# Reordering the opening of a two-block transformer kernel: modulation in column parts, four heads first, setup spread over the first batch

## The chip, the core and the metric

The kernel runs on one core of a Trainium2 chip. A core has five engines with a queue each: TensorE (PE, matrix products; PEld is its weight load), VectorE (DVE), ScalarE (ACT), GpSimd (POOL) and SyncE (SP), which here only issues DMA transfers. Each engine takes its instructions strictly in order; engines wait for one another by semaphores. The metric is the device time of one execution in microseconds (us), lower is better; the time of the kernel before is the median of three runs.

## The reference

Two transformer blocks run one after the other on x of shape 8 x 512 x 256 (8 batches, 512 tokens, 256 features, 16 heads), all in fp32. The opening, which the change touches, computes this of block 0:

```python
mod = jax.nn.silu(c) @ adaln_w.T + adaln_b            # 8 x 2304
shift_sa, scale_sa, gate_sa, shift_ca, scale_ca, gate_ca, shift_ff, scale_ff, gate_ff = jnp.split(mod, 9, axis=-1)
h = modulate(ln(x), shift_sa, scale_sa)               # x * (1 + scale) + shift
q = ln(_heads(h, H)) * qn_w + qn_b                    # head size 16, no projection
k = ln(_heads(h, H)) * kn_w + kn_b
v = _heads(h, H)
attn = jax.nn.softmax(jnp.einsum('bhqd,bhkd->bhqk', q, k) * scale, axis=-1)
x = x + gate_sa[:, None, :] * _unheads(jnp.einsum('bhqk,bhkd->bhqd', attn, v))
h = modulate(ln(x), shift_ca, scale_ca)
kv = brain_tokens @ cond_w.T + cond_b                 # 8 x 64 tokens of context
# cross attention of h with keys and values of kv, gated by gate_ca; then a gated feed-forward
```

Block 1 has self-attention with rotary positions and head size 64, cross attention with a layer-normed context (its keys and values, too, are made early, during block 0), and a feed-forward. Its two modulations are linear in the same condition vector: `g = c @ gw + gb`, four of them side by side (8 x 1024).

## The kernel before

x of all batches stays in SBUF, in 4 tiles of 128 tokens per batch. Block 0 is one software pipeline over **slots**: `run_blocks` (line 52) walks a list of `blocks`, and in each slot i emits first the scores of block i (`score`, 4 heads of one key tile: PE products into two pairs of PSUM banks, then two exponentials on ACT), then the values of block i - 1 (PE, into `ps_O`), then everything that `at(i, fn)` has registered for slot i, in the order of registration. A batch has 16 such self-attention blocks in a cycle of 18 slots (`CYCLE`); slots 9 and 13 of each cycle are left for the two blocks of cross attention of the batch before (`batch2`), and two cycles behind runs the feed-forward (`batch3`). So cycle 0 holds the self-attention of batch 0 and, in its gaps, the setup; cycle 1 holds batch 1, the cross attention of batch 0 and the keys of block 1 (`keys1`).

Heads go in groups of four: group g covers every second head of half c = g // 2 of the features (`c, par = divmod(g, 2)`). `queries_keys(g)` (line 472) transposes the normalized rows `z` on PE; ACT makes q, DVE makes k of it. It stands two slots before its group's first block. Its rows come from a chain of steps: `norm` (layer norm and modulation), `head_centre` (head mean subtracted, DVE), `head_var` (square on ACT, sum on DVE), `head_scale` (power -0.5 and product, POOL). For batch 0 these are registered in slots -1 to 1, for a later batch ten to four slots ahead of its first block, always ahead of the setup steps of the same slot, because the batches are registered first (line 690) and the setup after them.

PSUM: `bank_s` gives two buffers for scores; `bank_o` one for values; `bank_x` (line 99) hands out three banks in turn (two named ps_X, one ps_D) for everything else. Who asks for a bank waits until its last reader is done.

The setup: `linear_rows` (line 253) multiplies an 8-column stationary by 512 columns of weights, `to_columns` (260) transposes such rows in pieces of 128. `modulation` (slot 1), `context0` (3), `keys0` (5), `values0` (7 to 10), the layer norm of the context (5), `modulation1` (12) and `context1` (14) make the tables that cycle 1 needs. `awake(n)` (266) is n products of no use that keep PE busy while it waits for data. `rstd_of` (171) computes powers on POOL. The DRAM row `modd` holds the modulation, and `spread` (352) reads rows of it back, broadcast over the 128 partitions.

The order of PE, DVE, ACT and POOL inside `run_blocks` is the order of emission (`manual_schedule`, line 789); what stands ahead of it, and SP's queue everywhere, is ordered by the framework's planner. `keys1(p)` (730) stands in slots 20, 22, ... 34, and stores its result to DRAM at once (737); the cross attention's denominators take a way over DRAM on the same SP queue: `rec<-den` (616), `rec<-rec` (625), `rb<-rec` (627), after which DVE scales (630) what the output projection `w_o` reads on PE.

## Time and profile before

| what | value |
|---|---|
| median of 3 runs | 2475.15 us (2473.76 to 2475.49) |
| the profiled execution: its time, its span | 2477.8 us, 2476.0 us |
| granted TensorE clock, mean | 0.991 |
| PE, DVE, ACT, POOL busy, share of the span | 98%, 43%, 35%, 35% |
| first scores (slot 0) start | 25.07 us |
| slot 18 (first of cycle 1) starts | 100.40 us |
| clock at half in the first 200 us | 23.7 to 34.0, 85.2 to 92.0, 180.7 to 187.6 us |

How to read it: all times are from the span's start. In the timeline a row is start, duration, engine, line, operation, out<-in, shapes, count, and in brackets how long the engine had stood idle and what ended that. A row can merge several instructions of one kind. Line 109 is the helper `mm`, so matmuls are told apart by their tiles: `ps_S<-q,k` are scores, `ps_O<-p,h` values, `ps_X<-adaw,scT` the modulation. One fp32 product counts as two instructions. SPq rows are DMA issues. The clock is the share of the full TensorE clock that was granted.

### The profile page before, as it was taken

How to read it: one execution, taken by the hardware profiler on the slowest of the kernel's cores; microseconds unless marked ns; L12 is line 12 of the kernel's file. 1: busy time of each engine (PE TensorE's matmuls, PEld its weight loads, DVE VectorE, ACT ScalarE, POOL GpSimd, SP SyncE). 2: the span in 40 equal slices, each digit the busy share in tenths (PEclk: the TensorE clock that was granted, in tenths of full speed). 3: DMA queues.
4: the chain of work that ended last, by engine and by line, in shares of the span. 5: the costliest groups of instructions: out<-in, count | busy, mean ns of one | idle time of the engine just before them, and what ended most of it. 6: DMA issues, size and time to landing. Idle time of an engine off the chain costs nothing.

```text
span 2476.0 us, 28331 instructions
## 1 busy us (share of the span) xinstructions
PE 2414.9 (98%) x10938; PEld 1154.0 (47%) x10938; DVE 1070.0 (43%) x2073; ACT 876.7 (35%) x1115; POOL 857.8 (35%) x537
## 2 busy tenths in 40 slices
PE   8999999999999899999999999999999999999999
PEld 3323444434435543444444444444445555566666
DVE  4555435444434434343434343435343666651120
ACT  3555545555452124333333333333332121212221
POOL 3452322332301025343434343434343454441110
PEclk9999999999999999999999999999999999999999
DMA  5120000000002000000000000000113221211000
GB/s 183 36 82 24 17 11 12 21 11 12 13 11 79 10 1 23 19 18 19 18 18 19 18 19 18 19 18 18 36 61 95 66 67 51 76 42 41 18 21 23
DMA packets 84432, 84.33 MB, mean 34 GB/s; under 512 B 42400, under 2 KB 58720, under 8 KB 84280
## 3 DMA queue, kind: packets, MB, share of 16 engines
q1 hardware_dynamic: 83672, 81.88, 10.5%
q8 instruction: 88, 1.44, 0.2%
q10 hardware_dynamic: 616, 0.55, 0.1%
q14 instruction: 56, 0.46, 0.1%
HBM read 72.36 MB, written 10.04 MB: 33 GB/s over the span
## 4 chain that ended last, share of the span: by engine, by line
PE 93%; DVE 2%; ACT 2%; POOL 1%; issue 1%; DMA 0%; SPq 0%; POOLq 0%; DVEq 0%; ACTq 0%
PE ps_X L109 37%; PE ps_S L109 24%; PE ps_D L109 16%; PE ps_O L109 13%; PE ps_X L362 1%; ACT p L498 1%; DVE t L716 1%; POOL q L717 1%; PE ps_X L478 0%; PE ps_X L520 0%; ACT hT L363 0%; POOL rstd L469 0%; DVE t L713 0%; DVE st L183 0%; PE ps_D L478 0%
## 5 line engine op out<-in xcount | busy, mean ns | idle before, releaser
L109 PE MATMUL ps_S<-q,k 32*128 32x512 f32 (+1 forms) x3072 | 432.2, 627 | 7.0 <-ACT p L498 3.4
L886 ACT ACTIVATE p<-ps_S 128x1024 f32<-128x1024 f32 x256 | 248.2, 1022 | 522.2 <-PE ps_S L109 522.2
L498 ACT ACTIVATE p<-ps_S 128x1024 f32<-128x1024 f32 x256 | 248.2, 1021 | 259.6 <-PE ps_S L109 258.7
L109 PEld LDWEIGHTS ps_S<-q,k 32*128 32x128 f32 (+1 forms) x3072 | 160.2, 185 | 244.5 <-issue 134.3
L865 DVE TENSOR_TENSOR t<-ps_X,rope_c 128x512 f32<-128x512 f32 x126 | 87.1, 692 | 349.9 <-PE ps_X L109 349.9
L905 DVE TENSOR_TENSOR sm<-sm,p 128x1024 f32<-128x1024 f32 x128 | 191.4, 1539 | 59.0 <-ACT p L886 59.0
L175 POOL TENSOR_TENSOR rstd<-rstd,mhalf 128x4 f32<-128x4 f32 x49 | 49.8, 1016 | 392.4 <-DVE rstd L174 391.6
L868 POOL TENSOR_TENSOR q<-t 128x512 f32<-128x512 f32 x32 | 40.7, 1272 | 388.7 <-DVE t L866 388.7
L901 POOL TENSOR_TENSOR sm<-p 128x1024 f32<-128x1024 f32 x64 | 149.4, 2359 | 38.4 <-ACT p L886 38.4
L109 PE MATMUL ps_X<-hT,w 128*128 128x512 f32 x344 | 160.4, 601 | 1.6 <-DVE t L671 1.1
L717 POOL TENSOR_TENSOR q<-t,t 128x512 f32<-128x512 f32 x72 | 94.4, 1311 | 185.7 <-DVE t L716 170.9
L109 PE MATMUL ps_O<-p,h 128*32 128x512 f32 x1024 | 139.0, 615 | 0.5 <-ACT oT L511 0.5
L109 PE MATMUL ps_O<-p,v 128*64 128x512 f32 x512 | 138.0, 617 | 0.0
L109 PE MATMUL ps_D<-p,v 128*64 128x512 f32 x512 | 131.6, 592 | 0.0
L109 PE MATMUL ps_X<-hT,w_sa_wq 128*128 128x512 f32 x256 | 115.9, 595 | 3.0 <-ACT hT L363 3.0
L109 PE MATMUL ps_X<-w_sa_wv,hT 128*128 128x512 f32 x256 | 118.0, 604 | 0.0
L389 DVE TENSOR_TENSOR x<-ps_X,x 128x512 f32<-128x512 f32 x27 | 18.7, 691 | 225.0 <-PE ps_X L109 224.9
L109 PE MATMUL ps_X<-w_sa_wo,oT 128*128 128x256 f32 x512 | 114.5, 382 | 0.1
L109 PE MATMUL ps_X<-hT,w_sa_wk 128*128 128x512 f32 x248 | 112.4, 596 | 0.0
L109 PE MATMUL ps_S<-hT,w_ff_w 128*128 128x512 f32 x256 | 111.3, 592 | 0.0
L469 POOL TENSOR_TENSOR rstd<-var,mhalf 128x32 f32<-128x32 f32 (+1 forms) x17 | 87.3, 5134 | 68.3 <-ACT t L670 41.7
L109 PEld LDWEIGHTS ps_X<-w_sa_wo,oT 128*128 128x128 f32 x512 | 96.0, 190 | 24.2 <-issue 11.4
(252 smaller groups left out, 3542.4 us busy)
## 6 DMA issues: line engine op xcount, KB each, us to landing
rb<-rec SPq DMA_DIRECT2D x128, 128.0 KB
rb<-rec_d SPq DMA_DIRECT2D x124, 128.0 KB
x<-in_x_dram SPq DMA_DIRECT2D x8, 512.0 KB
rb<-rec SPq DMA_DIRECT2D x16, 256.0 KB
out_dram<-x SPq DMA_DIRECT2D x16, 256.0 KB
bc<-modd SPq DMA_DIRECT2D x8, 384.0 KB
gate<-modd SPq DMA_DIRECT2D x16, 128.0 KB
k_d<-q SPq DMA_DIRECT2D x8, 256.0 KB
```

The lines of the kernel that those rows point to most:

```text
L109: nc.tensor.matmul(o, lhsT, rhs, start=start, stop=stop)
L175: nc.gpsimd.tensor_tensor(r[:, :n], r[:, :n], mhalf[:, :n], ALU.pow)
L362: nc.tensor.transpose(ps[:, t * P : (t + 1) * P], z[:, t, k * P : (k + 1) * P], ident)
L469: nc.gpsimd.tensor_tensor(r, s["var", c][:, :, hd], half, ALU.pow)
L498: nc.scalar.activation(pr[u], pss[u], AF.Exp, scale=HD0 ** -0.5)
L716: nc.vector.tensor_tensor(t2[d], ps[src], sn[src].to_broadcast([64, *shape[1:]]), ALU.mult)
L717: nc.gpsimd.tensor_tensor(dst, t1, t2, ALU.add)
L865: nc.vector.tensor_tensor(c, ps, rope_c, ALU.mult)
L868: nc.gpsimd.tensor_tensor(r[0], ec, os, ALU.subtract)
L886: nc.scalar.activation(pr, pss[u], AF.Exp, scale=HD1 ** -0.5)
L901: nc.gpsimd.tensor_tensor(sm, s["p", g, 0, u], s["p", g, 1, u], ALU.add)
L905: nc.vector.tensor_tensor(s["sm", g, u], s["sm", g, u], s["p", g, t, u], ALU.add)
```

## The change

The opening is emitted in program order for PE, DVE, ACT and POOL (`ms` is entered ahead of it). x of batch 0 is loaded in four pieces, the first 512 columns of the modulation weights from ACT's queue, the rest and the biases (now in 4 + 1 pieces) from SP's. The first two modulation rows are made on PE for all 128 partitions at once (`sc0` is the condition of batch 0, repeated over 128 columns), bias and the added one included, where before a row was computed, added on DVE and spread by a product with ones. `awake` gets 6 and 16 products instead of 4 and 13.

Batch 0's steps up to the first scores are done for the first group of four heads alone, at half the width of before, with the last scaling on DVE; the other four heads of the half follow in slots 0 and 1, the second half in slots 2 to 4. `first_mod` is read until slot 2. `z` of batch 0 is filled with zeros as a whole.

`modulation` computes its first 2048 columns as four parts of 512 in four 32-column strips of PE (stationary `sc32`, 32 columns of which 8 are used); the last 256 are `modulation_end`; `modulation1` does the same with four parts of 256 and `c32`. Transposes, `context0`, `keys0` and `values0` become single pieces over slots 3 to 15. Fills on POOL move into slots 5 and 6. For batch 0 only the gate is spread, in slot 6; x of batch 1 is loaded earlier. Key stores of block 1 move from `keys1(p)` to three slots later, with three buffers instead of two, and `open_ff` (the feed-forward's weights) to two slots later.

The diff, cut to its core (`context0(m)`, `keys0(m)`, the columns' slices and the `par` argument of `head_centre` and `head_var` are as their names say):

```diff
     def load_rest():
         load_k(ctxT, a["ctxT"], 96)
         load_k(condw, a["cond_wT"], 96)
+        for j in range(4):
+            nc.sync.dma_start(gb[32 * j : 32 * j + B, :], a["gb_b"][:, D * j : D * j + D].to_broadcast([B, D]))
         nc.sync.dma_start(ctx_in, a["ctx"].rearrange("(t p) d -> p t d", p=P))
         load_k(wk0, a["wkT"])
+        load_x(1)
         load_k(wv0, a["wvT"])
         nc.sync.dma_start(rows, a["rows"].to_broadcast([P, 5 * D]))
-        nc.sync.dma_start(gb, a["gb_b"].to_broadcast([B, 4 * D]))
         load_k(gbw, a["gb_w"])
         load_k(w_q0, a["wqT"])
         load_k(w_o0, a["woT"])
-        for b in range(1, B):
+        for b in range(2, B):
             load_x(b)
 
-
-    scT = sp.tile([P, 2, B], F32, name="scT")
...
+    first_mod = bank_x()
+    ms = ExitStack()
+    ms.enter_context(tc.manual_schedule(engines={ENG.PE, ENG.DVE, ENG.Activation, ENG.Pool}))
+    nc.sync.dma_start(cT, a["cT"].rearrange("(k p) b -> p k b", p=P))
+    for k in range(2):
+        nc.scalar.dma_start(adaw[:, k, 0 : 2 * D], a["adaln_wT"][k * P : (k + 1) * P, 0 : 2 * D])
+    for t in range(NT):
+        nc.sync.dma_start(xs[0][:, t, :], a["x"][0][t * P : (t + 1) * P, :])
+    nc.vector.memset(mod, 0.0)
+    nc.vector.memset(gb, 0.0)
+    nc.gpsimd.memset(hs[0][:, :, :, HD0 + 1 : 32], 0.0)
+    nc.gpsimd.memset(hs[0][:, :, :, HD0 : HD0 + 1], 1.0)
+    nc.gpsimd.memset(sc32, 0.0)
+    nc.gpsimd.memset(c32, 0.0)
+    for j in range(4):
+        nc.sync.dma_start(mod[32 * j : 32 * j + B, 0 : 2 * D],
+                          a["adaln_b"][:, 2 * D * j : 2 * D * j + 2 * D].to_broadcast([B, 2 * D]))
+    nc.sync.dma_start(mod[0:B, 2 * D :], a["adaln_b"][:, 8 * D :].to_broadcast([B, D]))
+    nc.sync.dma_start(cols, a["cols"])
+    load_k(adaw[:, :, 2 * D :], a["adaln_wT"][:, 2 * D :])
+
     nc.scalar.activation(scT, cT, AF.Tanh, scale=0.5)
     nc.vector.scalar_tensor_tensor(scT, scT, 1.0, cT, ALU.add, ALU.mult)
     nc.vector.tensor_scalar_mul(scT, scT, 0.5)
-
-    def linear_rows(dst, xT, w, lo, n):
-
+    nc.vector.tensor_copy(sc0, scT[:, :, 0:1].to_broadcast([P, 2, P]))
+    awake(6)
+    for k in range(2):
+        mm(first_mod, sc0[:, k, :], adaw[:, k, 0 : 2 * D], k == 0, False)
+    mm(first_mod, ones, mod[0:1, 0 : 2 * D], False, False)
+    mm(first_mod[:, D : 2 * D], ones, chk[0:1].rearrange("p i c -> p (i c)"), False, True)
+    awake(16)
+
+    def modulation():
+
+        ps = bank_x()
+        for k in range(2):
+            for j in range(4):
+                mm(ps[32 * j : 32 * j + 32, :], sc32[:, k, :], adaw[:, k, 2 * D * j : 2 * D * j + 2 * D], k == 0, k == 1)
+        nc.vector.tensor_tensor(mod[:, 0 : 2 * D], ps, mod[:, 0 : 2 * D], ALU.add)
+        nc.vector.tensor_scalar_add(mod[0:B, D : 2 * D], mod[0:B, D : 2 * D], 1.0)
+        for j in range(4):
+            nc.sync.dma_start(modd[:, 2 * D * j : 2 * D * j + 2 * D], mod[32 * j : 32 * j + B, 0 : 2 * D])
+
+    def modulation_end():
+        ps = bank_x()
+        for k in range(2):
+            mm(ps[:32, :D], sc32[:, k, :], adaw[:, k, 8 * D :], k == 0, k == 1)
+        last = mod[0:32, 2 * D :]
+        nc.vector.tensor_tensor(last, ps[:32, :D], last, ALU.add)
+
+        nc.vector.tensor_scalar_mul(last, last, 0.5)
+        nc.sync.dma_start(modd[:, 8 * D :], mod[0:B, 2 * D :])
+
...
-    awake(4)
-    linear_rows(mod, scT, adaw, 0, 512)
-    nc.vector.tensor_scalar_add(mod[:, SC_SA : SC_SA + D], mod[:, SC_SA : SC_SA + D], 1.0)
-    first_mod = bank_x()
-    mm(first_mod, ones, mod[0:1, 0 : 2 * D])
-    linear_rows(mod, scT, adaw, 512, 256)
-    nc.sync.dma_start(modd[:, 0 : 3 * D], mod[:, 0 : 3 * D])
-    awake(13)
...
-    def modulation():
-        for lo in range(3 * D, 9 * D, 512):
-            linear_rows(mod, scT, adaw, lo, 512)
-
-        nc.vector.tensor_scalar_mul(mod[:, G_FF : G_FF + D], mod[:, G_FF : G_FF + D], 0.5)
-        nc.sync.dma_start(modd[:, 3 * D :], mod[:, 3 * D :])
-        to_columns(modT, mod, [lo + k * P for lo in (SH_CA, SC_CA, SH_FF, SC_FF) for k in range(2)])
-        for lo in (2, 6):
-            nc.vector.tensor_scalar_add(modT[:, lo : lo + 2, :], modT[:, lo : lo + 2, :], 1.0)
...
     def modulation1():
 
-        for lo in range(0, 4 * D, 512):
-            linear_rows(gb, cT, gbw, lo, 512)
-        gbT = sp.tile([P, 8, B], F32, name="gbT")
-        to_columns(gbT, gb, [k * P for k in range(8)])
+        ps = bank_x()
+        for k in range(2):
+            for j in range(4):
+                mm(ps[32 * j : 32 * j + 32, :D], c32[:, k, :], gbw[:, k, D * j : D * j + D], k == 0, k == 1)
+        nc.vector.tensor_tensor(gb, ps[:, :D], gb, ALU.add)
+
+    def modulation1_columns():
+        ps = bank_x()
+        for k in range(2):
+            nc.tensor.transpose(ps[:, k * P : (k + 1) * P], gb[:, k * P : (k + 1) * P], ident)
+        nc.vector.tensor_copy(gbT.rearrange("p (j k) b -> p k j b", j=4),
+                              ps[:, :D].rearrange("p (k j r) -> p k j r", k=2, j=4)[:, :, :, 0:B])
+
...
+        def first_modulated(c, par=None):
+
+            lv = parts(s["ln"], c, par)
+            n = lv.shape[2]
+            hv = s["hv"][:, :, 8 * c : 8 * c + 8] if par is None else s["hv"][:, :, 8 * c + par : 8 * c + 8 : 2]
+            sh, sc = (parts(first_mod[:, None, i * D : (i + 1) * D], c, par).to_broadcast([P, NT, n, HD0])
+                      for i in range(2))
+            nc.vector.tensor_tensor(lv, lv, sc, ALU.mult)
+            nc.vector.tensor_tensor(hv, lv, sh, ALU.add)
+
+        def head_rows():
+            s["z"] = wk.tile([P, NT, DX], F32, tag="zx", name="zx", bufs=1)
+            nc.gpsimd.memset(s["z"][:, :, D if b else 0 : DX], 0.0)
+
...
+        def head_scale(c, par=None, eng=None):
+            var, z = s["var", c, par], parts(s["z"][:, :, 0:D], c, par)
+            n = z.shape[2]
             half = mhalf[:, 0 : NT * n].rearrange("p (t h) -> p t h", t=NT)
-            nc.gpsimd.tensor_tensor(r, s["var", c][:, :, hd], half, ALU.pow)
-            nc.gpsimd.tensor_tensor(zv, zv, r[:, :, :, None].to_broadcast([P, NT, n, HD0]), ALU.mult)
+            nc.gpsimd.tensor_tensor(var, var, half, ALU.pow)
+            (eng or nc.gpsimd).tensor_tensor(z, z, var[:, :, :, None].to_broadcast([P, NT, n, HD0]), ALU.mult)
...
-                        at(-1, lambda: norm(0))
-                        at(-1, lambda: head_centre(0))
-                        at(-1, lambda: head_var(0))
-                        at(-1, lambda: head_scale(0, 0))
-                        at(0, lambda: head_scale(0, 1))
-                        at(0, lambda: norm(1))
-                        at(0, lambda: head_centre(1))
-                        at(1, lambda: head_var(1))
-                        at(1, lambda: head_scale(1))
+                        def before():
+                            head_rows()
+                            norm()
+                            nc.vector.tensor_copy(qk_cols, cols[:, 0:2])
+                            first_modulated(0, 0)
+                            head_centre(0, 0)
+                            head_var(0, 0)
+                            head_scale(0, 0, nc.vector)
+
+                        def gate():
+                            spread(s["bc"][:, 2 * D : 3 * D], b, G_SA, D)
+
+                        at(-1, before)
+                        at(0, lambda: first_modulated(0, 1))
+                        at(0, lambda: head_centre(0, 1))
+                        at(1, lambda: head_var(0, 1))
+                        at(1, lambda: head_scale(0, 1))
+                        at(2, lambda: first_modulated(1))
+                        at(3, lambda: head_centre(1))
+                        at(4, lambda: head_var(1))
+                        at(4, lambda: head_scale(1))
+                        at(6, gate)
...
+    at(0, lambda: nc.vector.tensor_copy(sc32[:, :, 0:B], scT))
     at(1, modulation)
-    at(3, context0)
-    at(5, keys0)
-    for t in range(4):
-        at(7 + t, lambda t=t: values0(t))
-    at(12, modulation1)
-    at(5, lambda: layernorm(ctx_z, ctx_in, EPS1, 4, CD))
-    at(14, context1)
+    at(3, modulation_columns)
+    at(3, modulation_end)
+    at(4, lambda: context0(0))
+    at(5, lambda: context0(1))
+    at(6, lambda: nc.gpsimd.memset(vb0, 0.0))
+    at(7, lambda: keys0(0))
+    at(8, lambda: keys0(1))
+    for h in hs[1:]:
+        at(5, lambda h=h: nc.gpsimd.memset(h[:, :, :, HD0 + 1 : 32], 0.0))
+        at(5, lambda h=h: nc.gpsimd.memset(h[:, :, :, HD0 : HD0 + 1], 1.0))
+    for t, i in enumerate((9, 9, 11, 12)):
+        at(i, lambda t=t: values0(t))
+    at(9, lambda: layernorm(ctx_z, ctx_in, EPS1, 4, CD))
+    at(12, lambda: nc.vector.tensor_copy(c32[:, :, 0:B], cT))
+    at(13, modulation1)
+    at(13, context1)
+    at(14, modulation1_columns)
+    at(15, modulation1_end)
...
-        q = kv1["pool"].tile([P, N], F32, tag="q", name="q")
+        kv1[p] = q = kv1["pool"].tile([P, N], F32, tag="q", name="q", bufs=3)
         rope_pair(kv1["pool"], ps.rearrange("p (j n) -> p j n", j=B), kv1["rope_c"][:, None, :], kv1["rope_s2"][:, None, :],
                   [P, B, T], q.rearrange("p (j n) -> p j n", j=B))
-        nc.sync.dma_start(k_d[:, p], q.rearrange("p (b t) -> p b t", b=B))
+
+    def store_keys1(p):
+        nc.sync.dma_start(k_d[:, p], kv1[p].rearrange("p (b t) -> p b t", b=B))
...
-    at(2 * CYCLE, open_ff)
+        at(CYCLE + 5 + 2 * p, lambda p=p: store_keys1(p))
+    at(2 * CYCLE + 2, open_ff)
```

## The prediction, made before the result was known

> **What bounds the kernel now.** I read the page first (busy shares, chain), then PE's busy time and granted clock in short windows, then the timeline of the first 190 us.

> ```profile
> PE 2414.9 (98%) x10938; PEld 1154.0 (47%) x10938; DVE 1070.0 (43%) x2073; ACT 876.7 (35%) x1115; POOL 857.8 (35%) x537
> ...
> PE 93%; DVE 2%; ACT 2%; POOL 1%; issue 1%; DMA 0%; SPq 0%; POOLq 0%; DVEq 0%; ACTq 0%
> ```

> PE bounds nearly all of it, so an edit of the opening pays only where PE stands still, runs at half clock, or does less. Windows (length; PE, PEld, DVE, ACT, POOL busy; granted clock; DMA):

> ```profile
> 20.31:23.72 3.41, 0.66 (x4) 0.42 (x4) 0.00 (x0) 0.33 (x1) 3.33 (x3) 1.00 0.97 345
> 23.72:27.13 3.41, 2.06 (x8) 0.52 (x8) 2.82 (x5) 0.45 (x1) 2.40 (x2) 0.50 1.04 384
> 27.14:30.55 3.41, 2.30 (x12) 1.00 (x8) 0.82 (x2) 2.10 (x3) 0.00 (x0) 0.50 1.10 351
> 81.75:85.16 3.41, 1.39 (x7) 0.36 (x5) 3.34 (x6) 0.00 (x0) 0.00 (x0) 1.00 0.00 0
> 85.16:88.58 3.42, 3.35 (x16) 1.21 (x20) 2.09 (x14) 0.83 (x2) 0.00 (x0) 0.50 0.00 0
> 180.74:187.56 6.82, 6.82 (x26) 2.76 (x26) 1.86 (x4) 2.65 (x3) 5.04 (x2) 0.50 1.04 366
> 1890.80:1894.21 3.41, 2.24 (x5) 0.93 (x6) 2.95 (x5) 0.00 (x0) 1.91 (x3) 1.00 0.00 0
> 1894.21:1897.62 3.41, 3.41 (x14) 2.25 (x13) 1.55 (x3) 1.61 (x2) 2.73 (x3) 1.00 0.02 4
> ```

> A window in which PE was busy 0.66 or 1.39 of 3.41 us is followed by clock 0.50; one with 2.24 is not. Half clock then lasts 6.8 to 10.2 us (23.72 to 33.96, 85.16 to 91.99, 180.74 to 187.56). The way to the first scores, in the timeline:

> ```profile
> 7.12 0.43 DVE L183 BATCH_NORM_STATS2 st<-x 128x6 f32<-128x256 f32 x1 [1.85 <-DMA x<-in_x_dram]
> ...
> 14.30 0.69 DVE L434 TENSOR_TENSOR ln<-ln,ps_X 128x512 f32<-128x512 f32 x1 [0.98 <-PE ps_X L109]
> ...
> 19.04 2.90 POOL L469 TENSOR_TENSOR rstd<-var,mhalf 128x16 f32<-128x16 f32 x1 [8.27 <-DVE var L460]
> ...
> 22.70 0.66 PE L478 MATMUL ps_X<-ident,zx 128*128 128x128 f32 x4 [3.06 <-POOL zx L470]
> ...
> 25.07 2.09 PE L109 MATMUL ps_S<-q,k 16*128 16x512 f32 x8 [1.72 <-DVE k L482]
> ```

> Call the scores of slot i S(i). S0 starts at 25.07; further down the same timeline S2 at 39.53, S12 at 76.23, S18 (the next batch) at 100.40. The two later stalls:

> ```profile
> 80.83 0.67 DVE L450 TENSOR_REDUCE mean<-h 128x32 f32<-128x512 f32 x1
> ...
> 84.63 0.41 PE L263 MATMUL ps_D<-ident,gb 8*128 8x8 f32 x4 [1.90 <-DVE gb L258]
> ...
> 171.53 2.50 POOL L717 TENSOR_TENSOR q<-t,t 128x512 f32<-128x512 f32 x2
> 172.84 0.33 SPq L737 DMA_DIRECT2D k_d<-q  x1
> 173.25 0.38 SPq L625 DMA_DIRECT2D rec<-rec  x1
> ...
> 179.82 2.06 PE L109 MATMUL ps_D<-w_o,oT 128*128 128x256 f32 x6 [3.23 <-DVE oT L630]
> ```

> At 84.63 PE waits for DVE, which is centring heads of the next batch. At 179.82 it waits for DVE's scaling, that for a DMA, and SP issued its forerunner only after a key store that waited for POOL.

> **The change part by part.** I laid the queues of PE, ACT, DVE and POOL out by hand from S0 to S18 in the listing's order, each instruction starting when its engine is free and its input there, with the durations of this execution: S 1.07 (2.04 where its second bank waits for the exponentials), values 1.0, exponentials 1.94, transposes 0.59, k 0.81, one centring 1.58. The old order, laid out alike, gives S18 at 102.5 against 100.40 in the trace: 2.1 too long over 75 us, so I take 1.0 off the new one.

> *1. To S0.* x arrives in four pieces of its own and behind less: 0.9 earlier by bytes ahead of it at 384 GB/s (estimate; bounds 0 and 1.7), so 6.2. Statistics of the last piece 0.6, then 1.32 over POOL and 1.38 scaling as before, with waits: normalized at 9.7. The modulation rows now come straight from PE: awake(6) is 12 instructions of 0.43 at half clock from 1.45 (the identity is done at 1.40), to 6.6; four of 0.43 to 0.86, two alike, two of 0.22 end at 9.2 to 10.5. So DVE's first product starts at 9.9, not 14.30. From there 10.77 led to S0; five DVE steps of half width cost 0.42, not 0.69 (1.35 less), the square 0.41, not 0.63, the scaling on DVE 0.42, not POOL's 0.62: 9.0. S0 at 18.9; awake(16), 32 x 0.216 = 6.9, ends at 16.1 to 17.4 where the transposes want 16.5. I take 19.0: **-6.1** (-4.5 to -6.6). POOL's fill of z (1088 columns at 1.77 per 2048: 0.95) and the two ACT issues ahead of its table load (0.43 each) lie under awake(6). SP issues 32 transfers to S0 instead of 26, at 0.43 about 14 us in all, under the same 19; none waits there for the modulation any more (8.6 us at line 278).

> *2. S0 to S2.* Modulation was 12 matmuls of 0.43 and transposes on PE; four column parts run together as the values do (8 instructions per 1.0), so 16 cost 2.0. S1 waits 2.2 for the exponentials, then 2.04 + 1.0 + 2.0: 7.2 instead of 14.46, **-7.2** at full clock. But between the first transposes (end 17.4) and S0 PE idles 1.7, then 1.1 before S1: a 3.41 window over this holds 1.1 to 1.8 busy, between the rows 1.39 and 2.24. I expect half clock (65 in 100; where the windows lie is not mine to choose): **+3.1** from the layout; 0 is the other end, 5.1 (10.24 us at half) the far one.
> [...]

> *3. S2 to S12.* Nine scores and nine values (18.6), four transposes (2.4) and setup (context 3.44, keys 3.44, three values0 2.58, columns 0.59, last part 0.86) make 31.9, about what it was. S11 waits for its exponentials as before (1.1 + 1.0). New are the waits: the transposes of slot 2 for POOL's 2.9 power of half block two (0.9), of slot 6 for its 5.44 one (1.1), and the second values0 of slot 9 for a bank that keys0(1) leaves only once DVE, busy with the next batch's layernorm (2.43 + 1.12 + 1.38), has read it (2.0). 31.9 + 6.1 = 38.0 instead of 36.7: **+1.3** (0 to +3).

> *4. S12 to S18.* A wait takes the place of the old one. c32's copy stands last in slot 12 on DVE: behind k (0.81), two centrings (3.16) and values0's four additions (1.2). modulation1, first in slot 13 after the values, needs it; the context transposes and S14 queue behind it. q ends 1.3 after the transposes; DVE's 5.3 then outlast PE's 0.86 + 1.0: PE idles **4.8** (3 to 5). That is over a window, so half clock follows as at 85.16, costing 2.7 (2.0 to 3.4). modulation1 itself falls from 8 x 0.43 to 1.0. Matmuls and usual waits 18.1 + 4.8 + 2.7 = 25.6 instead of 24.1: **+1.5** (-2.5 to +2.5).

> *5. Key stores.* Stored three slots later, they no longer stand before rec: it goes when DVE's reciprocal is done (170.57), not at 173.25. rb then lands about 2.7 earlier; PE waits 0.9 instead of 3.23 (2.3 saved), and no window falls under 1.4, so 6.82 at 0.50, wholly busy, costs 3.4 less: **-5.7** (0 to -6.6). The third buffer of q lets POOL write before the store; open_ff two slots later leaves six slots of over 5 us to up(0), which used hT from 209.20, 33 us after the weights' issue at 176.17. From here to 766 PE has no gap over 0.3, so what is gained stays.

> *At nothing:* the fill of vb0 (1.80) and of the second h on POOL in slots 5 and 6, behind the scaling of slot 4 and before values0 in slot 9; gate's spread in slot 6, used in slot 19; the five stores of modulation, behind the loads on SP, first read in slot 8; w_ck's load, freed by DVE's last setup product in slot 15, some 8 us before S18 as now (92.36). Without that cover they would come onto POOL's and SP's queues, where the power of slot 14 (two of 5.44) is next in line and its transposes have under 1 us to spare.

> *Sum:* -6.1 - 7.2 + 3.1 + 1.3 + 1.5 - 5.7 - 1.0 = -14.1. The profiled execution took 2477.8 (span 2476.0), 2.65 over the median: 2463.7, and on the median's footing **2461.0**.

> **Rivals.** *A: no half clock at the start* (window falls well; 1.7 idle only): 2461.0 - 3.1 = 2457.9. *B: DVE keeps up*: c32 comes early enough that PE stops under 2 us, no half clock at slot 13; against it k alone waits for ACT. 2.8 + 2.7 better: 2455.5, with A 2452.4. *C: the key-store stall stays*, since POOL's power (5.42) is the same and SP may find another wait: +5.7, 2466.7; with the late ends of 1 (+1.6) and 3 (+1.7), 2470.0. *D: within 0.2%*: C so, with the far ends of 2 (+2.0) and 4 (+1.0) as well, 2473. *E, slower:* the clock stays at half. Windows with 2.06 and 2.30 busy did not lift it. If cycle 0's sparse slots (S on 16 rows, waits for ACT) keep it there, each window costs up to 1.7; nine windows, 31 us or S0 to S8, eat the 14.1, and twelve give 2461.0 + 20.4 = 2481. Against it: at half clock the same work fills windows, as 30.55 to 33.96 did.

> **How the numbers follow.** Forecast with half clock at the start and the c32 wait 40, A 22, B 13, C 12, D 8, E 5 in 100. Leaving out E, D's upper half and a little of B's far end: 2450 to 2470. 0.2% (4.95 us) is about what a measurement of this kernel tells from no change: under 2470.2 is faster 0.87, D same 0.08, E slower 0.05.

> **What would show it.** S0 at 18.9 to 19.8; PE idle near 1.7 before it, and whether clock 0.50 follows; modulation's 16 matmuls in about 2.0; PE waiting 3 to 5 us for DVE's c32 before modulation1, with 0.50 after it; S18 near 92; no wait of 3 us before w_o's matmuls, and full clock after them. I am wrong if DVE's order in slot 12 is not the listing's, if ACT's queue brings the weights later than 7 us, or if rec waits for POOL again.

## The result, and the profile after

The changed kernel takes 2471.45 us (median of 20 executions, 2465.9 to 2478.21). The kernel before, executed beside it, takes 2477.91 (20 executions, 2473.76 to 2484.3). The ratio is 0.9972, 95% interval 0.9963 to 0.9980: faster by 0.28%, 6.5 us, where 14.1 were forecast. The median of three from which the forecast was counted, 2475.15, lies 2.8 under that of the twenty, so the forecast is compared as a difference. The executions spread over 12 us.

The profiled execution took 2471.62, span 2469.8, clock 0.990. The page's first and fourth part:

```profile
PE 2410.8 (98%) x10952; PEld 1154.1 (47%) x10952; DVE 1065.5 (43%) x2083; ACT 877.3 (36%) x1116; POOL 856.6 (35%) x538
...
PE 92%; DVE 2%; POOL 2%; issue 2%; ACT 1%; DMA 0%; SPq 0%; POOLq 0%; DVEq 0%; ACTq 0%
```

PE bounds it as before. The way to the first scores, and slots 13 to 15, in the timeline (start, duration, engine, line, operation, count, idle before and what ended it):

```profile
9.98 0.42 DVE L477 TENSOR_TENSOR ln<-ln,ps_X 128x256 f32<-128x256 f32 x1
...
13.23 2.90 POOL L506 TENSOR_TENSOR var<-var,mhalf 128x16 f32<-128x16 f32 x1 [4.77 <-DVE var L500]
...
19.10 1.38 PE L109 MATMUL ps_S<-q,k 16*128 16x512 f32 x8 [1.72 <-DVE k L519]
...
75.78 1.19 DVE L342 TENSOR_TENSOR vb<-ps_D,rows 64x128 f32<-64x128 f32 x4
...
76.98 0.18 DVE L759 COPY c<-cT 128x16 f32<-128x16 f32 x1
...
77.25 1.35 PE L109 MATMUL ps_X<-gbw,c 128*32 128x256 f32 x16 [4.57 <-issue]
...
83.16 2.38 PE L109 MATMUL ps_S<-q,k 16*128 16x512 f32 x8 [0.37 <-ACT p L535]
```

S0 starts at 19.10 instead of 25.07, and PE waits 4.57 us for c32's copy, which DVE reaches at 76.98. PE's windows (length; PE, PEld, DVE, ACT, POOL busy; granted clock; DMA) show what follows:

```profile
16.46:19.88 3.42, 1.71 (x15) 0.90 (x13) 1.70 (x5) 0.78 (x1) 0.00 (x0) 1.00 1.08 374
19.88:23.29 3.41, 2.32 (x10) 1.00 (x8) 1.09 (x4) 1.94 (x2) 0.00 (x0) 0.50 1.00 377
...
74.49:77.90 3.41, 0.65 (x12) 0.50 (x16) 3.25 (x11) 1.18 (x2) 0.00 (x0) 1.00 0.01 2
77.90:81.32 3.42, 3.42 (x20) 1.97 (x16) 2.85 (x6) 0.00 (x0) 3.28 (x1) 0.50 0.02 5
81.32:84.73 3.41, 3.04 (x22) 1.24 (x14) 2.03 (x9) 2.28 (x3) 3.33 (x3) 1.00 0.00 0
84.73:88.14 3.41, 3.41 (x16) 0.72 (x16) 1.60 (x11) 1.71 (x2) 3.41 (x1) 0.50 0.10 26
...
98.38:101.80 3.42, 3.42 (x18) 0.72 (x16) 0.00 (x0) 2.48 (x3) 0.00 (x0) 0.50 0.00 0
101.80:105.21 3.41, 3.41 (x16) 0.92 (x12) 0.00 (x0) 1.94 (x2) 0.00 (x0) 0.50 0.00 0
105.21:108.62 3.41, 3.41 (x23) 1.35 (x23) 1.00 (x5) 2.14 (x3) 2.27 (x1) 1.00 0.02 5
```

The clock is half from 19.88 to 30.12, from 77.90 to 81.32, and then from 84.73 to 105.21, six windows in which PE was occupied throughout. The window ahead of these six had PE occupied for 3.04 of 3.41 us and no gap above 0.37. Where the gain stands, by the starts of slots:

| slot | before | after | gain |
|---|---|---|---|
| S0 | 25.07 | 19.10 | 6.0 |
| S2 | 39.53 | 29.77 | 9.8 |
| S12 | 76.23 | 68.10 | 8.1 |
| S18 | 100.40 | 96.15 | 4.3 |
| S20 | 106.27 | 105.25 | 1.0 |
| S37 | 173.19 | 171.86 | 1.3 |
| S39 | 188.91 | 184.72 | 4.2 |

Nearly all is lost between S12 and S20. From S37 to S39 it grows by 2.9, because the clock was not halved near 180 this time. The stall there is still in place:

```profile
170.21 2.50 POOL L780 TENSOR_TENSOR q<-t,t 128x512 f32<-128x512 f32 x2
...
171.52 0.32 SPq L802 DMA_DIRECT2D k_d<-q  x1
...
171.93 0.38 SPq L676 DMA_DIRECT2D rec<-rec  x1
...
172.74 0.32 SPq L802 DMA_DIRECT2D k_d<-q  x1
...
178.85 1.56 PE L109 MATMUL ps_X<-w_o,oT 128*128 128x256 f32 x6 [3.58 <-DVE oT L681]
```

SP issues a key store ahead of rec, as before, and PE waits 3.58 (3.23 before). SP's order at this place is the same in the traces of both kernels: rec<-den, k_d<-q, rec<-rec, k_d<-q, rb<-rec. All eight key stores have been issued by 172.74, so these two are the last two, which the changed listing puts behind rec (slots 35 and 37 against 34).

### The profile page after: what moved, and what is told of

Read it like the earlier page. It is cut to its first block, busy times and chain, and to the rows that moved or that the text cites. A ratio compares the mean times of both kernels' runs of the same rounds, so it can differ in the third digit from the quotient of the medians.

```text
span 2469.8 us, 28399 instructions
## 1 busy us (share of the span) xinstructions
PE 2410.8 (98%) x10952; PEld 1154.1 (47%) x10952; DVE 1065.5 (43%) x2083; ACT 877.3 (36%) x1116; POOL 856.6 (35%) x538
## 3 DMA queue, kind: packets, MB, share of 16 engines
q10 hardware_dynamic: 904, 1.07, 0.2%
## 4 chain that ended last, share of the span: by engine, by line
PE 92%; DVE 2%; POOL 2%; issue 2%; ACT 1%; DMA 0%; SPq 0%; POOLq 0%; DVEq 0%; ACTq 0%
PE ps_X L109 38%; PE ps_S L109 23%; PE ps_D L109 15%; PE ps_O L109 13%; PE ps_X L392 1%; POOL var L506 1%; DVE t L779 1%; ACT p L535 1%; POOL q L780 1%; PE ps_X L515 0%; PE ps_D L392 0%; ACT hT L393 0%; PE ps_X L557 0%; DVE t L776 0%; DVE st L183 0%
## 5 line engine op out<-in xcount | busy, mean ns | idle before, releaser
L109 PE MATMUL ps_S<-q,k 32*128 32x512 f32 (+1 forms) x3072 | 431.3, 630 | 7.4 <-ACT p L535 4.4
L109 PEld LDWEIGHTS ps_S<-q,k 32*128 32x128 f32 (+1 forms) x3072 | 159.3, 186 | 245.5 <-issue 132.8
L109 PE MATMUL ps_X<-hT,w 128*128 128x512 f32 x344 | 162.2, 606 | 0.9 <-ACT hT L393 0.4
L967 POOL TENSOR_TENSOR sm<-p 128x1024 f32<-128x1024 f32 x64 | 149.3, 2355 | 38.2 <-ACT p L952 38.2
L109 PE MATMUL ps_O<-p,h 128*32 128x512 f32 x1024 | 141.6, 626 | 0.0
L109 PE MATMUL ps_O<-p,v 128*64 128x512 f32 x512 | 138.0, 617 | 0.0
L109 PE MATMUL ps_D<-p,v 128*64 128x512 f32 x512 | 131.6, 592 | 0.0
L109 PE MATMUL ps_X<-hT,w_sa_wq 128*128 128x512 f32 x256 | 115.9, 595 | 3.0 <-ACT hT L393 3.0
L109 PE MATMUL ps_X<-w_sa_wv,hT 128*128 128x512 f32 x256 | 118.0, 604 | 0.0
L109 PE MATMUL ps_X<-w_sa_wo,oT 128*128 128x256 f32 x512 | 114.5, 382 | 0.1
L506 POOL TENSOR_TENSOR var<-var,mhalf 128x32 f32<-128x32 f32 (+1 forms) x17 | 87.7, 5160 | 75.5 <-ACT t L721 41.7
L109 PE MATMUL ps_X<-hT,w_sa_wk 128*128 128x512 f32 x248 | 112.4, 596 | 0.0
L109 PE MATMUL ps_S<-hT,w_ff_w 128*128 128x512 f32 x256 | 111.3, 592 | 0.0
L109 PEld LDWEIGHTS ps_X<-w_sa_wo,oT 128*128 128x128 f32 x512 | 96.0, 190 | 24.2 <-issue 11.4
```

The lines of the kernel that those rows point to most:

```text
L109: nc.tensor.matmul(o, lhsT, rhs, start=start, stop=stop)
L506: nc.gpsimd.tensor_tensor(var, var, half, ALU.pow)
L967: nc.gpsimd.tensor_tensor(sm, s["p", g, 0, u], s["p", g, 1, u], ALU.add)
```

## The experiments

Two theories. **W/H, on the clock:** the missing gain went into half clock after S12; W says that the wait for c32 is its cause, H that slots 14 to 20 hold the clock down whatever went before. **C, on the stores:** moving them in the listing did not move them in SP's queue.

All variants are edits of the changed kernel. The half-clock time is a mean over all of a variant's executions, twice (1 - granted clock) times the span. S18 is that of the profiled execution. Ratios are to the kernel before on the same chip. Only the intervals of best and best_fill lie clear of the changed kernel's; those of c32_early_ctx_late, fill_wait and store_pool just reach into it, and the other variants are not told apart from it in time.

| kernel | median us | ratio, 95% | half-clock time | S18 |
|---|---|---|---|---|
| before (75 executions beside the variants) | 2476.65 to 2477.21 | 1 | 38.2 | 100.40 |
| changed | 2471.45 | 0.9972 (0.9963-0.9980) | 45.9 | 96.15 |
| c32_early | 2473.57 | 0.9979 (0.9970-0.9988) | 54.8 | 97.39 |
| c32_early_ctx_late | 2464.93 | 0.9950 (0.9937-0.9963) | 37.4 | 93.52 |
| fill_wait | 2465.34 | 0.9951 (0.9938-0.9964) | 31.5 | 89.60 |
| store_pool | 2467.52 | 0.9952 (0.9938-0.9967) | 42.8 | 100.35 |
| store_old | 2471.77 | 0.9979 (0.9969-0.9989) | 49.0 | 97.60 |
| awake_start | 2471.05 | 0.9980 (0.9969-0.9991) | 44.1 | 97.21 |
| dense_slots | 2471.47 | 0.9988 (0.9978-0.9998) | 44.5 | 93.64 |
| slot14_dense | 2469.94 | 0.9978 (0.9968-0.9987) | 39.5 | 94.08 |
| values_apart | 2471.25 | 0.9976 (0.9965-0.9987) | 52.3 | 92.88 |
| heads_together | 2472.70 | 0.9986 (0.9977-0.9995) | 52.3 | 98.20 |
| best | 2454.32 | 0.9906 (0.9892-0.9920) | 19.6 | 84.84 |
| best_fill | 2458.03 | 0.9929 (0.9916-0.9942) | 22.6 | 87.17 |

**fill_wait: keep the wait, take the idle time away.**

```diff
+    at(13, lambda: awake(8))
     at(13, modulation1)
```

> The changed kernel with eight products of no use (16 instructions of 0.216, 3.5 us) put ahead of modulation1: the wait for the copy of c32 stays, but PE idles only about 1.1 of the 4.57 us. This parts the wait from the clock. Theory W says that the idle time halves the clock from 77.90 and, again, from 84.73: without it modulation1 still starts at 77.25, S14 near 79.5 instead of 80.41, S18 near 90.4 instead of 96.15 (10.9 from S14 at full clock), time 5 to 6 lower, near 2466. Rival H (the sparse slots hold the clock down by themselves): S18 stays within 1.5 of 96.15 and the time within 2 of 2471.5.

```profile
72.43 3.72 PE L109 MATMUL ps_S<-chk,ident 128*128 128x256 f32 x16
77.03 1.07 PE L109 MATMUL ps_X<-gbw,c 128*32 128x256 f32 x16 [0.87 <-DVE c L759]
```

Two windows of PE behind it:

```profile
77.21:80.62 3.41, 3.41 (x37) 1.92 (x30) 3.16 (x7) 0.35 (x1) 2.76 (x1) 1.00 0.00 0
80.62:84.03 3.41, 3.04 (x20) 0.88 (x18) 3.02 (x15) 3.04 (x4) 3.33 (x2) 1.00 0.00 0
```

modulation1 still starts at 77.03, 9.1 after S12 as in the changed kernel, and nothing is half between 30 and 169. S12 to S18 takes 21.7 instead of 28.1, S12 to S20 27.5 instead of 37.2. The time is 6.1 lower. W holds: what the wait cost beyond itself was the clock, and that was most of the loss. The filler also puts full-array products into these windows, so this run alone does not part idle time from sparse work. Its window from 80.62, occupied for 3.04 us, kept the clock; the changed kernel's window from 81.32, occupied for 3.04 us as well, did not.

**c32_early: take the wait away by its source.**

```diff
-    at(12, lambda: nc.vector.tensor_copy(c32[:, :, 0:B], cT))
+    at(4, lambda: nc.vector.tensor_copy(c32[:, :, 0:B], cT))
```

> One line differs from the changed kernel: the copy that fills c32 is registered in slot 4 instead of slot 12. Theory W (the missing gain lies in PE's 4.57 us wait for this copy before modulation1 and in the half clock that follows it): modulation1 starts near 72.9 instead of 77.25. A smaller wait takes its place: the second half of context1 needs the bank that DVE reads for values0(3) until 76.96, so PE stops for about 2.8 there; S14 near 78.2 instead of 80.41. If the clock stays full from there, S14 to S18 takes 10.9 (2.75 for S14 to S15, and 8.18 for S15 to S18 as in the kernel before) and S18 starts near 89 instead of 96.15; time 7 lower, 2464. Rival H (a stop of 2.8 is enough to halve the clock, and slots 14 to 20 then hold it there): S18 at 92 to 94, time 2467 to 2470. Rival N (the copy is not what modulation1 waits for): the wait stays at 4.5 and the time at 2471.5.

```profile
77.33 0.64 PE L378 MATMUL ps_X<-ident,ctx_z 128*96 128x128 f32 x4
80.48 0.61 PE L378 MATMUL ps_D<-ident,ctx_z 128*96 128x128 f32 x4 [2.50 <-DVE vb L342]
```

A miss for W's number: after the new wait of 2.50 (2.8 expected), with PE busy for 1.08 us of the window from 78.15, the clock was half from 81.56, and it stayed so for nine windows, to 112.28. The time is no lower than that of the changed kernel. H's number was nearer, but still too low. This execution was at half clock from 61.1 to 74.7 as well, well ahead of the new wait; S12 to S18 takes 27.9, as long as in the changed kernel.

**c32_early_ctx_late: take the second wait away, too.**

```diff
-    at(13, context1)
-    at(14, modulation1_columns)
-    at(15, modulation1_end)
+    at(15, modulation1_columns)
+    at(15, context1)
+    at(16, modulation1_end)
```

(with the copy in slot 4)

> As the run with the early copy, and context1 and modulation1_columns moved to slot 15, modulation1_end to slot 16, so that nothing in slot 13 needs DVE's late additions. Theory W: PE has no stop over 1 us from S12 to S14; modulation1 ends near 73.7 and S14 follows at once, 6.7 before 80.41. What is late next is POOL's power for batch 1 (78.04 to 83.46, its product done at 84.60), which the transposes of slot 16 need: PE waits 2 to 4 us there, S18 near 88.5 (96.15 in the changed kernel), time near 2464. Rival H (slots 14 to 20 are short of work for PE, so the clock halves in them whatever goes before): half clock for 7 to 20 us between 74 and 105, S18 at 91 to 95, time 2467 to 2470.

2464.93, as W had it, though what was late next was not POOL's power: S15 waited 1.71 for its banks, whose exponentials stood on ACT behind squares that wait for DVE. The clock was half from 81.75 to 88.57 only. It came back after the window with the ten transposes of the context and of gb, which now stand in slot 15 among the scores.

**dense_slots, slot14_dense: what holds the clock down.** The profiles so far suggested that occupation is not what counts (3.04 us kept the clock in fill_wait and lost it in the changed kernel). For every window of 3.41 us I summed over PE's instructions rows/128 x columns/128 x duration, counted from its start, and divided by 3.41: the share of the array at work. It is a way of counting, with two choices in it. Fewer than 32 columns count as 32. 256 moving columns count 0.427 us at half clock, at which such products follow one another in the trace of the kernel before, and half of that, 0.213, at full clock (they follow at 0.216). Scores on 16 rows count an eighth each, four at a time a half: in the trace of the changed kernel four of them start within 0.02 us. That the next window's clock goes with this share, and not with occupied time, is theory U, and slot14_dense was made to try it: the window 81.32 to 84.73 of the changed kernel has a share of 0.35, two products on the full array (four instructions) add 0.25, and by U no half clock follows it then. (dense_slots ran before it; its rival U is another theory.)

```diff
+    for i in (15, 16, 17, 18):
+        at(i, lambda: awake_x(2))          # dense_slots
...
+    at(14, lambda: awake_x(2))             # slot14_dense
```

(`awake_x` is `awake` with a bank from `bank_x`)

> The changed kernel with two products of no use on all 128 rows (4 instructions, 0.86 us at full clock, 1.7 at half) at the end of each of the slots 15 to 18. The wait for c32 stays. Theory L (at half clock, windows that hold mostly scores on 16 rows and values do not lift it, though PE is busy throughout; full products in the window do): the half clock after 78 ends within two windows, 6.8 us in a stretch, instead of 20.48; the added work costs 3.4 at full clock and up to 2 more, the lifted clock gives back up to 6.8, so the time lies between 2469 and 2473, and S18 to S20 takes 6 to 8 instead of 9.1. Rival U (full occupation does not matter): half clock for 15 us or more in a stretch, S20 5 to 7 later than 105.25, time 2476 to 2479.

> The changed kernel with two products of no use on the full array (4 instructions, 0.86 us) at the end of slot 14. [...] The stretch of 20.48 us is gone, S18 starts between 89 and 92 instead of 96.15, time 4 to 6 lower than 2471.45, near 2466. Rival L (half clock is started by the idle time before modulation1 alone, and the sparse slots merely keep it): a stretch of over 13 us after 77 remains, time 2471 to 2473.

dense_slots had one half window (77.42 to 80.84) after its wait of 4.57 in the profiled execution, and S20 at 99.50 instead of 105.25. But its executions range from 2469.18 to 2479.38 with 29.6 to 59.5 us of half clock, hardly less on the mean than the changed kernel's: inconclusive. slot14_dense is clear on the clock, in its profiled execution. awake_start (below) has the window grid within 0.2 us of it, and half clock from 75.6 to 82.4 ahead of it as well. These are three windows of slot14_dense, and then the three of awake_start:

```profile
78.83:82.24 3.41, 3.41 (x24) 2.03 (x20) 2.27 (x5) 0.00 (x0) 3.41 (x1) 0.50 0.00 0
82.24:85.66 3.42, 2.38 (x18) 1.32 (x10) 2.12 (x11) 1.94 (x2) 3.34 (x3) 1.00 0.00 0
85.66:89.07 3.41, 3.23 (x22) 0.77 (x20) 1.28 (x9) 1.94 (x2) 3.41 (x1) 1.00 0.18 46
```

```profile
79.03:82.44 3.41, 3.41 (x20) 1.97 (x16) 2.22 (x4) 0.00 (x0) 3.41 (x1) 0.50 0.00 0
82.44:85.85 3.41, 3.04 (x22) 1.24 (x14) 1.99 (x12) 2.31 (x3) 3.33 (x3) 1.00 0.00 0
85.85:89.27 3.42, 3.42 (x16) 0.72 (x16) 1.04 (x7) 1.68 (x2) 3.42 (x1) 0.50 0.23 53
```

In the middle window PE was occupied for 2.38 us in slot14_dense, and the clock stayed; for 3.04 us in awake_start, and it fell; the shares of the array are 0.49 and 0.36. With this window filled, the stretch of 20.48 us is gone from the profiled execution, though the wait for c32 stands: the first half clock came with the wait, the long one after the sparse window, and only the long one went with the filler. The median is 1.5 lower where 4 to 6 were expected, and the ratio, 0.9978, is no better than the changed kernel's 0.9972: no gain in time is shown. The filler itself waited 1.04 for its bank, and the half clock from the wait for c32 is still there. So theory U was right on the clock after this one window, in one profiled execution of each kernel, and the expectation was wrong on what that is worth here.

**awake_start: no idle time ahead of S0 and S1.**

```diff
+    at(-1, lambda: awake(4))
     at(-1, load_rest)
+    at(0, lambda: awake_x(3))
```

> The changed kernel with four products of no use (8 instructions of 0.216) between the first transposes and S0, where PE idles 1.72, and three (1.3 us) between S0 and S1, where it idles 1.09. Theory W for the opening (the idle 1.72 and 1.09 in one window of 3.41 are what halves the clock): no half clock between 17 and 31; S0 and S1 start as before (19.1 to 19.4, 21.6), modulation's 16 instructions take 2.0 instead of 3.64, S2 starts near 26.2 instead of 29.77; time 3 to 3.5 lower, near 2468. Rival H (the scores on 16 rows halve it all the same): S2 within 1 of 29.77 and the time within 1 of 2471.5. Rival B (the added products delay S0 or S1): S1 later than 22.3.

```profile
24.77 1.90 PE L109 MATMUL ps_X<-adaw,sc 128*32 128x512 f32 x16
26.60 1.14 PE L109 MATMUL ps_S<-q,k 16*128 16x512 f32 x8
...
30.10 0.66 PE L521 MATMUL ps_X<-ident,zx 128*128 128x128 f32 x4 [1.36 <-POOL zx L513]
```

The half clock of the start is gone, modulation takes 1.90 instead of 3.64, and S2 starts 3.2 earlier. Then the gain goes: 1.36 to POOL's power ahead of the transposes of slot 2, the rest to half clock from 61.96 to 68.79. S12 starts at 68.41 (68.10), and the time is the same. The 3.2 us gained here were lost again to those 6.83 us of half clock and the wait of 1.36.

**values_apart, heads_together: two parts of the opening.**

```diff
-    for t, i in enumerate((9, 9, 11, 12)):
+    for t, i in enumerate((9, 10, 11, 12)):   # values_apart
...
-                            first_modulated(0, 0)
-                            head_centre(0, 0)
-                            head_var(0, 0)
+                            first_modulated(0)  # heads_together: all eight heads ahead of S0
+                            head_centre(0)
+                            head_var(0)
+                            for e in range(2):
+                                s["var", 0, e] = s["var", 0, None][:, :, e:8:2]
...
-                        at(0, lambda: first_modulated(0, 1))
-                        at(0, lambda: head_centre(0, 1))
-                        at(1, lambda: head_var(0, 1))
```

> The changed kernel with the second and third values0 in slots 10 and 11, so that the four stand in 9, 10, 11 and 12. The wait of the second for keys0's bank falls from 1.57 to about 0.5, and S11's wait for its exponentials from 1.17 to 0.3, since values0 fills it: S12 near 66.2 instead of 68.10. By theory U the windows around 58 to 62 then have over 0.37 in every position of the grid, so the half clock from 61 to 75 that followed in several executions of the variants so far is gone; time 2 to 4 lower than 2471.45, and the highest execution under 2476. Rival (the gain is eaten by the wait for c32, which grows by as much, since DVE and not PE sets when that copy is done): modulation1 still at 77, time within 1 of 2471.45.

> The changed kernel with one part of its opening undone: modulation, centring and variance of batch 0's first half are done for its eight heads at once ahead of S0, as in the kernel before, instead of four heads alone. By step 1 of the prediction five steps of DVE cost 0.69 instead of 0.42 and the square on ACT 0.63 instead of 0.41: S0 at 20.7 instead of 19.1, and PE idles 1.6 more ahead of the first transposes. Theory: the loss of 1.6 stays to S12 and the time is 1 to 2 higher, near 2473. Rival (the four other heads cost DVE as much in slots 0 and 1, so that S1 or the transposes of slot 2 wait less now): S12 within 0.5 of 68.10 and the time within 1 of 2471.45.

values_apart: the wait falls from 1.57 to 0.49, S12 starts at 63.88, 4.2 earlier, and no half clock follows near 61. modulation1 comes at 73.40, after a wait of 4.33, and not at 77, so its rival's mechanism fails, though the time that it named came. The half clock after it, 71.3 to 78.1 and 81.5 to 102.0, takes the gain all the same: the executions run from 2459.98 to 2475.56, and the median is the changed kernel's. heads_together: S0 at 20.46 (20.7 expected), S12 at 69.58, time 1.25 higher, inside the expected 1 to 2, though by the intervals that is no more than the measurement tells.

**store_old, store_pool: the key stores.**

```diff
-        at(CYCLE + 5 + 2 * p, lambda p=p: store_keys1(p))
+        nc.gpsimd.dma_start(k_d[:, p], q.rearrange("p (b t) -> p b t", b=B))   # store_pool, in keys1
+        nc.sync.dma_start(k_d[:, p], q.rearrange("p (b t) -> p b t", b=B))     # store_old, in keys1
```

> The changed kernel with its part on the key stores undone: each store stands inside keys1 again, with two buffers of q, and open_ff at slot 36. Theory C (moving the stores three slots later in the listing changes nothing in SP's queue, in which k_d<-q still stands ahead of rec<-rec): PE's wait ahead of w_o's matmuls stays between 2.7 and 3.6 us, the step from S37 to S38 between 7.8 and 8.7 (8.48 with the part, 8.62 in the kernel before), time within 1.5 of 2471.5. Rival M (the part did move something, and only the half clock hides it): the wait grows to 5 or more, or q's missing third buffer holds POOL, and the time rises by 2 to 6.

> The changed kernel with the eight stores of block 1's keys issued from POOL's own queue, right behind the addition that makes them, instead of from SP's. Theory C (the stall ahead of w_o's matmuls stays because SP's queue still holds a key store ahead of rec<-rec: 171.52 against 171.93, and both wait for POOL's addition, done at 171.49): rec goes when DVE's reciprocal is done, near 169.3; rb lands 2.6 earlier, DVE scales near 175.5 instead of 178.10, PE's wait falls from 3.58 to about 1.0, time 2.0 to 2.6 lower, near 2469. Rival P (POOL is the bound: the issues cost POOL over 1 us each, ahead of the powers that the transposes of slots 32 to 38 need): the wait moves to those transposes and the time stays within 1 of 2471.5 or rises.

(store_old takes back the third buffer of q and open_ff's slot, too; in both, the separate store at `CYCLE + 5 + 2 * p` is gone.) The timeline of store_old:

```profile
172.48 0.32 SPq L801 DMA_DIRECT2D k_d<-q  x1
172.89 0.38 SPq L676 DMA_DIRECT2D rec<-rec  x1
173.71 0.32 SPq L801 DMA_DIRECT2D k_d<-q  x1
...
179.78 1.56 PE L109 MATMUL ps_X<-w_o,oT 128*128 128x256 f32 x6 [3.10 <-DVE oT L681]
```

With the part undone the order is the same, the wait is 3.10, S37 to S38 takes 8.00 (8.48 with it), and the time 2471.77: the part shows no worth. With the stores on POOL's queue (the timeline of store_pool):

```profile
173.25 0.33 SPq L676 DMA_DIRECT2D rec<-rec  x1
174.43 1.28 POOL L780 TENSOR_TENSOR q<-t,t 128x512 f32<-128x512 f32 x1
...
176.00 0.62 POOL L801 DMA_DIRECT2D k_d<-q  x1 [0.30 <-POOL q L780]
...
179.66 1.56 PE L109 MATMUL ps_X<-w_o,oT 128*128 128x256 f32 x6 [0.41 <-DVE oT L681]
```

rec goes before POOL's addition, PE waits 0.41, S37 to S38 takes 5.30 instead of 8.48, and the median is 3.9 lower, over six executions from 2460.44 to 2472.95. POOL pays 0.6 for each issue; S18 to S37 takes 75.5 (75.7 in the changed kernel), so PE does not pay for it. Theory C holds.

**best, best_fill: the parts together.** `best` joins c32_early_ctx_late, store_pool, awake_start and values_apart; best_fill adds `at(14, lambda: awake_x(4))`.

> The changed kernel with four edits together: c32's copy in slot 4 with context1 and modulation1_columns in slot 15 (modulation1_end in 16), the key stores on POOL's queue, the products of no use around S0, and the second and third values0 a slot later and alone (slots 9, 10, 11, 12), so that the second waits less for keys0's bank (1.57). If the four gains add: 6.5 from the copy and the context (2464.93 against 2471.45), 3.9 from the stores (2467.52), 3 from the start, 1.5 from the values (and none of the half clock from 61 to 75 that followed that wait in some executions), so 2471.45 - 14.9 = 2456.5. Rival S (they share the half clock that they save): 2459 to 2462.

> The fastest variant so far (2454.32) with four products of no use at the end of its slot 14 (8 instructions, 1.73 us), where PE idles 2.07 for S15's banks, held by exponentials that stand on ACT behind squares which wait for DVE. Theory U: the window 69.6 to 73.0 had a share under 0.37 and the clock was half from 73.03 to 79.86; with the products it is not: S16 near 76.5 instead of 79.30, time 2.5 to 3.4 lower, near 2451.5. Rival D (DVE and POOL, not PE, set when slot 16 can go on: POOL's power of batch 1): the transposes of slot 16 wait instead, S18 within 1 of 84.84, time within 1 of 2454.3.

The span and mean granted clock of best (0.990 in the changed kernel):

```profile
core 0: 2452.4 us, clock 0.996
```

best beats both kernels: 2454.32, 17.1 under the changed one (2456.5 expected). c32_early_ctx_late (6.5) and store_pool (3.9) would add up to 10.4, so values_apart and awake_start, worth nothing alone, seem to count once most of the half clock behind them is gone (19.6 us are left, in every execution). No run joins the first two without the others, so this last step is argued, not shown. best_fill is a miss: its products waited 4.86 for a bank that DVE had still to read, which cost more than the 2.07 they were to fill.

## Why the prediction was right or wrong

*Step 1 is right.* DVE's first product at 9.98 (9.9), S0 at 19.10 (19.0), PE idle 1.72 ahead of it.

*Step 2 is right, with the half clock as long as at its far end.* S0 to S2 took 10.67 (7.2 + 3.1 = 10.3). awake_start shows the same stretch at full clock: 6.94, so the 10.24 us at half clock cost 3.7 (5.1 at the far end). The half clock that was given 65 in 100 came: the window 16.46 to 19.88, with PE busy for 1.71 us and no gap above 1.72, was followed by it, as 81.75 to 85.16 of the kernel before was, with 1.39 and no gap above 1.90.

*Step 3 is right.* S2 to S12 took 38.33 (38.0), with the waits named: 0.83 for POOL in slot 6, 1.57 for keys0's bank; the 0.9 in slot 2 came only in awake_start, where PE was early.

*Step 4 is the term that failed.* Its wait was right, cause and size (4.57 against 4.8). Its half clock was put at 2.7, one period as after 85.16 in the kernel before. By fill_wait it costs 6.4 to S18 and 9.6 to S20. The reason for rejecting rival E, "at half clock the same work fills windows", is what fell: after five windows that PE filled (shares of the array 0.55 to 0.71) the clock was still half, after the sixth, with 0.81, full. The prediction read the clock off the time that PE was busy in a window (1.39 too little, 2.24 enough). By that the window from 81.32, busy for 3.04, was safe; it had 0.35 of the array at work, and the clock fell. The window 30.55 to 33.96 that was cited had modulation's products in it beside the values; slots 15 to 20 have only scores on 16 rows, values and a few transposes. Its share, with two products of 8 columns in it, was 0.61, though, no more than those of the five, so the share does not say why the clock rose after it and not after them. E's long half clock came, for six windows where E had counted nine to twelve. The edge of 0.37 in the expectations of values_apart and best_fill is shown by no run: in the traces of the two kernels windows with 0.24 to 0.36 were followed by full clock, others with 0.06 to 0.35 by half.

*Step 5 failed, as rival C said, for a reason that the prediction did not have.* It took the listing's order for SP's, although the section on the kernel before says that the planner orders SP's queue. The store stayed ahead of rec in the queue that was built. Of 5.7 the stall's 2.3 did not come. The 3.4 for the clock came in the profiled execution, but it was not the change's: the window before 180.30 held six full-array products, a share of 0.37 with PE busy for 1.45 us, and kept the clock, while fill_wait and slot14_dense, with the same stall, were half from 169.4 and 174.4.

*The sum.* Forecast was 12.3 us less half clock (4.0 at the start: 10.24 to twice 3.1; 1.4 after modulation1: 6.83 to twice 2.7; 6.8 near 184). On the mean of all executions there were 7.7 more (45.9 against 38.2). A line through the 20 executions of the changed kernel has 0.33 us of time per us of half clock, so these 20.0 make 6.6, and the stall 2.3. The 1.0 that was taken off because the old order came out too long by hand had nothing to answer it, either: at full clock steps 2 and 3 took 6.94 and 38.33, against 7.2 and 38.0. Together 9.9, against 7.6 missing: the account closes to 2.3 us, and medians over such a spread allow no more.

## What to carry to other kernels

Where PE lives on products that use few rows, look at the share of the array per window beside occupied time (0.49 with 2.38 us occupied kept the clock, 0.36 with 3.04 lost it), and try dense work (transposes, setup) among the sparse slots rather than ahead of them: in c32_early_ctx_late the half clock ended at 88.57, after the window with the ten transposes. An earlier start can be taken back by half clock that comes later: awake_start's S2 was 3.2 us earlier, its S12 was not. A filler product should write a bank that is already free, or it is a wait itself (4.86 us in best_fill, 1.04 in slot14_dense). Before counting on a moved DMA, read the order of the queue that was built: the line that issues the key store was moved, and the store still went at 171.52, ahead of rec at 171.93.

## What the runs showed of the hardware

| clock in the window | clock in the next | kernel before | changed kernel |
|---|---|---|---|
| full | half | 0.13 (0.66) at 20.31; 0.06 (1.39) at 81.75; 0.24 (0.92) at 177.32 | 0.32 (1.71) at 16.46; 0.18 (0.65) at 74.49; 0.35 (3.04) at 81.32 |
| full | full | 0.38 (3.41) at 10.07; 0.27 (3.42) at 33.96; 0.24 (3.10) at 37.38; 0.34 (3.41) at 78.34 | 0.36 (2.24) at 60.84; 0.38 (1.61) at 71.08; 0.37 (1.45) at 176.89 |
| half | half | 0.25 (2.07) at 23.72; 0.21 (2.30) at 27.14; 0.63 (3.35) at 85.16; 0.60 (3.41) at 180.74 | 0.20 (2.32) at 19.88; 0.72 (3.41) at 23.29; 0.64 (3.41) at 84.73; 0.71 (3.42) at 88.14; 0.61 (3.41) at 91.56; 0.55 (3.41) at 94.97; 0.69 (3.42) at 98.38 |
| half | full | 0.61 (3.41) at 30.55; 0.69 (3.41) at 88.58; 0.94 (3.41) at 184.15 | 0.90 (3.42) at 26.70; 0.62 (3.42) at 77.90; 0.81 (3.41) at 101.80 |

Occupied time does not part the windows at full clock: 1.45 and 1.61 us kept it, 1.71 and 3.04 lost it. Nor does the share do so for all: 0.24, 0.27 and 0.34 kept it in the kernel before. These three windows hold products of 8 columns, where the way of counting is unsure; of the others the two that lie closest, 0.352 (lost, from 81.32) and 0.356 (kept, from 60.84), differ by less than the counting can tell. At half clock 0.62 (from 77.90) was followed by full clock and 0.64 to 0.71 (from 84.73, 98.38 and 88.14) by half in the same trace; 0.69 was followed by full clock in the kernel before (88.58) and by half in the changed one (98.38). Near 830 us, where PE has no scores or values, half clock went on after windows with 0.48 (from 829.27, kernel before) and 0.51 (from 825.42, changed kernel). All this is a reading of two traces; only slot14_dense tried it directly.

The half periods of the changed kernel up to 2440 us are 10.24, 3.41, 20.48, 6.83 and 3.41. Where the windows fall differs from profile to profile (one starts at 77.90 in the changed kernel, at 78.83 in slot14_dense). The same program had between 34.5 and 69.3 us of half clock, and one profile shows one of these cases; that the place of the windows makes this difference is the author's estimate, not shown. What decides at half clock between shares of 0.61 and 0.72 stays open.
